# A ResNet-with-attention pair on one NeuronCore: another queue for the first input, lent rooms for weights, another projection order, halved last products

## The chip, the cores and the metric

The kernel runs on one core of a Trainium2 chip. The metric is the device time of one execution in microseconds (us), as the median of three runs. One more execution is recorded by the hardware profiler; its trace has a span of its own, which starts and ends with the first and last instruction of the program.

## The reference

Two bottleneck blocks on 16 images of 1024 channels and 32 x 32 pixels, all float32. The first block has local self-attention over 3 x 3 neighbours (32 heads of 8 channels) in its middle, the second has a plain 3 x 3 convolution:

```
# block 0
h = relu(bn(conv1x1(x, w_conv1)))                     # 1024 -> 256
q, k, v = relu(bn(conv1x1(h, wq))), relu(bn(conv1x1(h, wk))), bn(conv1x1(h, wv))
attn = softmax_k(einsum('bgdhw,bgdkhw->bgkhw', q, unfold3x3(k) + pos))
a = relu(bn(einsum('bgdkhw,bgkhw->bgdhw', unfold3x3(v), attn)))
x1 = relu(bn(conv1x1(a, w_conv3)) + x)                # 256 -> 1024
# block 1
y = relu(bn(conv1x1(x1, w1)))                         # 1024 -> 256
y = relu(bn(conv3x3(y, w2)))                          # 256 -> 256
out = relu(bn(conv1x1(y, w3)) + x1)                   # 256 -> 1024
```

## The kernel before, in words

An image is a sequence of stages, and the stages of the 16 images stand in one list (`stages`, made from the words `P0 P1 ... U15`). C is the first 1x1 convolution (`first_conv`, L1058), Q and V are the projections (`project`, L443), F is the last 1x1 of block 0 fused with the first 1x1 of block 1 (`fused`), W is the 3x3 convolution of four images by Winograd's form (`winograd_conv`), U is the last 1x1 (`last_sum`; for images 12 to 15 `late_sums` with Strassen's seven products on a quarter of the output each, `Pair`). `P0` stands for C0 Q0 V0. The list begins `P0 P1 P2 P3 C4 F0 Q4 V4 F1 P5 P6 F2 P7 F3 C8 Q8 W0 V8 ...` and ends `F12 F13 F14 U10:0123 F15 U10:4567 U11:01234 W12 U11:567 U12 U13 U14 U15`.

TensorE (PE) runs the stages in that order. A float32 matrix product appears in the trace as two MATMUL passes, so 6240 passes are 3120 products. PSUM holds four tiles of 128 x 1024 (`psum`, `bufs=4`), which ScalarE empties (L423 for F and U, L471 for q, k and v, L512 for the position product) and also fills in advance with the residual (L395, `seed`). VectorE computes the attention (L603 to L682), Winograd's transforms (L734 to L745), and in W the sums of the products. The engines execute what they are given in program order, each its own.

What VectorE does between the stages, and with it the order on the other engines' queues, is written out by hand: `ORDER` has a word for each part of a stage, and each letter of a word emits one step: `j` a step of attention, `e` the exponentials (on ScalarE, L642), `f` a step of the transforms in front (at first Winograd's transform of the weights, `winograd_weights`), `m` a move, `a` ReLU of attention's result (L709), `w` ReLU of Winograd's result (L893). Before any `e`, `j` steps have made the logits; L635 subtracts their maximum.

DMAs are issued from three queues. SyncE (SP) loads weights (`more_weights`, L131) and stores k and v with a halo (L483), transformed weights (`uw`, L289) and transformed images (`v`, L770). GpSimd (POOL) loads x, residuals and transformed images (`more_loads`, L344) and stores results (L424). ScalarE loads the parameters `par` (L92), and that is its first instruction. All of x, the two halves of the first chunk among them, is loaded by GpSimd's queue.

Weights have five rooms of 128 x 1024 (`wpool`). A new piece is asked for when an old one is used up (`done_with`), from a list in the order of use (`queue`). The 3x3 convolution has 18 pieces U of 512 KB, and PE takes each for 8 products.

In `project` the order is k, q, v by halves n = 0, 1. For `together(b)` (images from 4 on, where V follows Q at once) it is k0 k1 q0 q1 v0, then the position product (L504), then v1; else k0 q0 q1 k1, position product, v0 v1. Where a fused stage or U follows, the two residual seeds of that stage are put into PSUM tiles before v0/position and before v1.

At the very end `late_sums` runs `Pair` objects, one per quarter of the output channels. For the last two pairs (`end`) products 2 and 3 go to PSUM banks that already hold the rest of the sum, so that only the last step of the result (bias and ReLU) and the store follow.

Of the kernel before, what the change touches and what calls it, by code (L numbers as in the profile page):

```python
# [72 lines left out]
def sa_bottleneck_kernel(ctx: ExitStack, tc: tile.TileContext, x, w1t, wqkvt, w3t, u1t, u2t, u3t, params, out):  # L73
# [15 lines left out]


    par = const.tile([P, _NPAR], F32, tag="par", name="par")
    nc.scalar.dma_start(par, params)  # L92


    uw = dram.tile([NI, 3, P, NW, 2, WID], F32, tag="uw", name="uw")
# [18 lines left out]
    def more_weights():  # L114

        if not queue:
            return
        key = name, of, half = queue.pop(0)
        t = wpool.tile([P, HW], F32, tag="w", name=f"{name}{half}_{of[0]}")
        src = source(name, half)  # L120
        n, k = src.shape[-1], 1
        for d in src.shape[1:-1]:
            k *= d
        view = t[:, : k * n].rearrange("p (c n) -> p c n", n=n)
        if len(src.shape) == 4:
            view = t.rearrange("p (m j o) -> p m j o", m=NW, j=2)
        if of[1] == 0 and name == "w1":
            for part in (slice(0, 1), slice(1, k)) if half == 0 else (slice(0, k),):
                nc.sync.dma_start(view[:, part], src[:, part])
        else:  # L130
            nc.sync.dma_start(view, src)  # L131
        pieces[key] = view

    def done_with(key):

        if last_use[key] == now[0]:
            more_weights()

    now = [0]

# [172 lines left out]
    def more_loads():  # L313

        while loads and live[0] < CHUNKS + RESULTS - 1:
            kind, b, c = loads[0]
            late = kind == "r" and b >= B - NK

            spare = kind == "x" and b < 2 and c >= CHUNKS
            if live[0] >= CHUNKS and not (kind == "x" and b < 2) and not (late and late_rooms):  # L320
                return
            if kind == "V":

                if forms.get((b, c[1] == 2), 0) < NK:
                    return
                src = form_room(b)[c[0], c[1]].rearrange("p k j e -> p (k j e)")
            elif kind == "r":
                if (b, c) not in stored:
                    return
                src = stored[b, c]  # L330
            else:
                src = x[b, c * P : (c + 1) * P, :]
            name = f"{kind}_{b}_{c}".translate(str.maketrans(" ,", "__", "()"))
            if late and live[0] >= CHUNKS:
                t = late_of[loads[0]] = late_rooms.pop(0)
                live[0] -= 1
            elif spare:
                t = rpool.tile([P, HW], F32, tag="r", name=name)
            else:
                t = xpool.tile([P, NK * 2 * PART], F32, tag="x", name=name)  # L340
                t = t if kind == "V" else t[:, :HW]

            for part in ((slice(0, HALF), slice(HALF, HW)) if loads[0] == ("x", 0, 0) else (slice(None),)):
                nc.gpsimd.dma_start(t[:, part], src[:, part])  # L344
            loaded[loads.pop(0)] = t
            live[0] += 1

# [543 lines left out]
    def finish_winograd(b, n):  # L891
# [4 lines left out]
        )  # L896

    ORDER = (
        ". . f . ff f . fff . . ff f . ff . . . ff ffff j ff jj j . j . j . . jj jj . jj jj . . . e j j j j "
        "jj j j jj j j j . jjjj . . j j . j j . a j j j j j j e j . . jj jj . jjj jmj j . . j . jj . j . . jj "  # L900
        ". . f aj ff . . . jf . . . j fjj jj j fj j . ej jj j jm j . mfj . . j j . jj . jj j f f f f . jf . j "
        "f j fj j . . j j j j ajj j . j e . jjj m jj j m j j j . j j . jjj . jj . . . jj j . j jf . f f . afj "
        "j f j . . . jj ffj e . jjj j mmjj . j . jj . . . . . jj f j f . f fff . jjjf . . . . jj . . j j . . "
        ". . . j . . . . . . . . . . j jw j j jw j j ejj j j . j jmm j jww . j j jj . jj . j j j j . j j jww "
        ". jj j j j jejj ja mjww m j j j . j . jj . j . j . jj j . jja . j jj . . j j j jj . j jejj m . jjm . "
        ". j ja j . f . ff f j f j . fjf . . . . . jj j jj j . ff a f f j f j . fjf . . . . j . j jjj . f f f "
        "f j j ff jejj . jf m . ff . ffm . f f j fj . j j . j . j j j j jj j . j j . j . . jj . . j . j . . . "
        "j . . . . . . . . . . . jwj j je jjjw . mj mj j . jj . . j jww . j jjj . j j . j j j . j . jj jww j "
        "jj j ejajj . mj jj w mw jj . j . j j j jj j . . . j j j a j j j j jj . j jje jj j . jm m j . j j j . "
        ". j f f f f j f j . fjjjf . . . j j . j j f f ff . aj . f j . . . j fj jjf j j je a jjj . . j mj . . "  # L910
        "j . jmj . j . jj j . jjf . . f . f f jf . . jff . jf . ff . . . f fff j j j . . . j jj j j . . . . j "
        ". . . . . . . . j . . ejj j mwwj m jjj . . . j j j . j jww jj j . j jj . . j j j . jjaj . j jww jej "
        "jj m . j mj . j ja . . j jj . j j jj j j . . . . j j . jj . j j ajj j j je jjj . j j . . . j . j jj "
        ". . j j jf . f . ff j f . ffffffffwf a . ff . . w . . . . . . . ff . . fff . . . . . . . ff ff . . . "
        "f . f . f . . . . . . . . . . . . . . . . . . . ww w w w w . w . w . . . . . . . . . "
    )

    class Side:
# [100 lines left out]

    def together(b):  # L1020
        at = [(kind, c) for kind, c, of in stages].index(("qk", b))
        return b >= 4 and stages[at + 1][0] == "v"

    def weights_of_stage(kind, b, of):
        if kind == "conv1":
# [134 lines left out]
    def late_weights():  # L1160
# [4 lines left out]
        for half in range(2):  # L1165
# [7 lines left out]
        blocks["s"] = s  # L1173
        rooms = [
            apool.tile([P] + shape, F32, tag=tag, name=tag).rearrange("p d w -> p (d w)")
            for tag, shape in (("bnv", [HEAD_DIM, HALO]), ("bnk", [HEAD_DIM, HALO]), ("qc", [HEAD_DIM, JPIX]),
                               ("pc", [NPOS, JPIX]))
        ]
        rooms.append(kp.rearrange("p n r w -> p (n r w)"))
        hidden_ = vh.rearrange("p r w -> p (r w)")  # L1180
        for k, t in enumerate(rooms[:3] + rooms[4:]):
# [21 lines left out]
    class Pair:  # L1203
# [18 lines left out]
        def product(self, i):  # L1222
# [8 lines left out]
            nc.tensor.matmul(ps, w, by, start=i in (1, 2, 7) and not (i == 2 and self.end), stop=True, skip_group_check=True)  # L1231
            if i == 1 or (i == 2 and not self.end):
                self.add(0, 0, ps)
                if self.end:
                    nc.scalar.activation(self.banks[2], self.r[0][:, :HALF], AF.Identity)
            elif i == 6:
                self.add(1, 0, ps)
            elif i == 5:
                if self.end:
                    self.add(0, 1, ps)  # L1240
                    if self.last:
                        nc.vector.tensor_copy(self.banks[3], self.r[0][:, HALF:])
                    else:
                        nc.scalar.activation(self.banks[3], self.r[0][:, HALF:], AF.Identity)
                    self.add(1, 1, ps)
                else:
                    self.add(1, 1, ps)
                    self.add(0, 1, ps)
# [3 lines left out]
                self.add(1, 0, ps)  # L1252
            elif i == 3 and not self.end:
                nc.scalar.activation(self.r[0][:, HALF:], ps, AF.Identity)

        def result(self, m):
            o = 2 * self.q + m
# [4 lines left out]
            if self.end:  # L1262
# [3 lines left out]
                    nc.scalar.activation(t_, r_, RELU, bias=shift, scale=1.0)  # L1266
                    nc.gpsimd.dma_start(to, t)
                elif m == 1:
                    nc.scalar.activation(t_[:, two], r_[:, two], RELU, bias=shift, scale=1.0)
                    nc.vector.tensor_scalar(t_[:, one], r_[:, one], shift, 0.0, ALU.add, ALU.max)  # L1270
                    nc.sync.dma_start(to, t)
                elif not self.last:
                    for i, part in ((2, one), (3, two)):
                        ps = self.banks[i].rearrange("p (j n) -> p j n", j=2)
                        nc.scalar.activation(t_[:, part], ps, RELU, bias=shift, scale=1.0)
                    nc.sync.dma_start(to, t)
                else:
                    ps = [self.banks[i].rearrange("p (j n) -> p j n", j=2) for i in (2, 3)]
                    nc.scalar.activation(t_[:, one], ps[0], RELU, bias=shift, scale=1.0)
                    nc.vector.tensor_scalar(t_[:, two], ps[1], shift, 0.0, ALU.add, ALU.max)  # L1280
                    nc.scalar.dma_start(to[: P // 2], t[: P // 2])
                    nc.sync.dma_start(to[P // 2 :], t[P // 2 :])
            else:
                nc.scalar.activation(t_, r_, RELU, bias=shift, scale=1.0)
                nc.gpsimd.dma_start(to, t)
# [4 lines left out]
    def late_sums():  # L1290
# [8 lines left out]
        for b in range(B - NK, B):  # L1299
            steps = iter(())  # L1300
            for q in range(NC // 2):
# [5 lines left out]
                if last_one:  # L1307
                    last_one.product(5)
                    for m in (1,) if last_one.end else range(2):
                        last_one.result(m)  # L1310
                if this.last:
                    order = (6, 7, 5, 4)
                elif this.end:
                    order = (7, 6, 4)
# [4 lines left out]
                if this.last:  # L1319
                    last_one.product(2)  # L1320
                    last_one.product(3)
                    this.result(1)
                    last_one.result(0)
                    this.product(2)
                    this.product(3)
                    this.result(0)
                else:
                    for _ in range((0, 1, 2, 1)[q]):
                        next(steps, None)
# [8 lines left out]
    def run(at):  # L1338
# [3 lines left out]
        for after in stages[at : at + 3]:  # L1342
            if after[0] == "fused":
                next_fused[0] = after[1]
                break
        fetch_attended()
        if kind == "fused":
            parts, count = fused(b, of, then), 2 * NC
        elif kind == "u3" and b >= B - NK:
# [35 lines left out]
    def at_first():  # L1385
        more_weights()
        more_loads()
        more_weights()
        norms()
        load_taps(0)  # L1390
# [55 lines left out]
```

## Time and profile before

| | |
|---|---|
| median of 3 runs | 2380.18 us (2379.92 to 2381.85) |
| profiled execution, its own time | 2377.51 us |
| its span in the trace | 2375.8 us, at a granted TensorE clock of 0.999 |
| PE busy | 2350.4 us (99%), 6240 passes |
| DVE (VectorE) busy | 2163.3 us (91%) |
| ACT (ScalarE) busy | 932.8 us (39%) |
| POOL busy | 492.0 us (21%) |
| DMA | 691.11 MB, 291 GB/s over the span |

PE is the engine named in 88% of the chain that ends last. Its busy time counts matmul passes whose ends are modelled. The step from the start of one pass to the start of the next is the better measure: 0.429 us for a pass of 512 columns and 0.216 us for one of 256, wherever nothing holds PE up. A longer step is a stall, and the stalls can be added up from the timeline.

### The profile page before, as it was taken

Reading aid. Unit: us, or ns where it says so; the run is one execution under the profiler, and the core shown is the slowest. Engines: PE = TensorE matmul, PEld = TensorE weight load, DVE = VectorE, ACT = ScalarE, POOL = GpSimd, SP = SyncE. Lnnn points to the kernel's source line nnn. Section 1 sums busy time; section 2 is a strip of 40 time slices with the busy share of each in tenths; the row PEclk is TensorE's granted clock in tenths of the full one; section 3 lists DMA queues with packets and bytes.
Section 4 is the critical chain, followed back from the end, with each engine's and each line's share of the span. In section 5 each row is a group of like instructions: output and inputs, shape, how many; then the busy total and the mean of one; then the engine's idle time right before and its main releaser. Section 6 shows DMA issues by size and latency. Waiting matters only on the chain.

```text
span 2375.8 us, 18829 instructions
## 1 busy us (share of the span) xinstructions
PE 2350.4 (99%) x6240; PEld 1142.1 (48%) x6240; DVE 2163.3 (91%) x1784; ACT 932.8 (39%) x889; POOL 492.0 (21%) x903
## 2 busy tenths in 40 slices
PE   8999999999999999999999999999999999999998
PEld 3444444444476444444466444444467444444843
DVE  4989999999989999999899989999989989975687
ACT  3322342323122574433122574324222463354277
POOL 3211121212121232111111232112111231111222
PEclk9999999999999999999999999999999999999999
DMA  9967786877797998687888998678788897698988
GB/s 341 382 223 265 276 276 248 279 279 263 268 329 243 338 396 316 221 266 238 254 310 271 326 381 326 219 274 288 261 293 295 309 369 248 214 345 288 332 296 292
DMA packets 294769, 691.11 MB, mean 291 GB/s; under 512 B 20752, under 2 KB 164624, under 8 KB 285968
## 3 DMA queue, kind: packets, MB, share of 16 engines
q0 software_dynamic: 120192, 472.19, 54.6%
q1 hardware_dynamic: 174256, 217.41, 28.1%
q8 instruction: 50, 0.82, 0.1%
q14 instruction: 47, 0.39, 0.0%
q10 hardware_dynamic: 224, 0.31, 0.0%
HBM read 414.79 MB, written 275.03 MB: 290 GB/s over the span
## 4 chain that ended last, share of the span: by engine, by line
PE 88%; DVE 6%; DMA 2%; ACT 1%; issue 0%; SPq 0%; ACTq 0%; DVEq 0%
PE ps L372 35%; PE ps L404 28%; PE ps L458 13%; PE ps L805 8%; PE ps L1231 4%; DMA U<-uw 2%; DVE prod L603 1%; DVE acc L660 1%; DVE acc L678 1%; DVE prod L608 0%; ACT kp L471 0%; DMA v<-v 0%; PE ps L504 0%; DVE form L734 0%; DVE z L831 0%
## 5 line engine op out<-in xcount | busy, mean ns | idle before, releaser
L372 PE MATMUL ps<-result,u 128*128 128x512 f32 x1024 | 458.4, 593 | 0.1
L404 PE MATMUL ps<-a,w 128*128 128x512 f32 x1024 | 457.8, 593 | 0.0
L372 PE MATMUL ps<-x,w 128*128 128x512 f32 x1024 | 444.3, 595 | 7.8 <-DMA x<-in_x_dram 7.5
L660 DVE TENSOR_TENSOR acc<-e,bnv 128x2048 f32<-128x2048 f32 x144 | 327.5, 2283 | 27.5 <-ACT e L642 24.4
L404 PE MATMUL ps<-y,u 128*128 128x512 f32 x768 | 331.1, 592 | 0.0
L603 DVE TENSOR_TENSOR prod<-qc,bnk 128x2048 f32<-128x2048 f32 x144 | 324.1, 2287 | 1.8
L423 ACT ACTIVATE result<-ps,par 128x1024 f32<-128x1024 f32 x128 | 142.4, 1113 | 452.6 <-PE ps L404 379.6
L372 PEld LDWEIGHTS ps<-x,w 128*128 128x128 f32 x1024 | 195.6, 191 | 253.2 <-issue 242.8
L372 PEld LDWEIGHTS ps<-result,u 128*128 128x128 f32 x1024 | 194.7, 190 | 245.5 <-issue 236.4
L404 PEld LDWEIGHTS ps<-a,w 128*128 128x128 f32 x1024 | 195.0, 190 | 244.5 <-issue 243.7
L678 DVE TENSOR_TENSOR acc<-acc 128x2048 f32<-128x2048 f32 x128 | 293.4, 2292 | 4.4
L404 PEld LDWEIGHTS ps<-y,u 128*128 128x128 f32 x768 | 146.3, 190 | 182.9 <-issue 180.9
L458 PE MATMUL ps<-h,wqk 128*128 128x512 f32 x512 | 222.3, 593 | 0.0
L424 POOL DMA_DIRECT2D r<-result x128 | 68.7, 537 | 600.7 <-ACT result L423 574.3
L608 DVE TENSOR_TENSOR prod<-prod 128x2048 f32<-128x2048 f32 (+1 forms) x80 | 166.2, 2077 | 2.3
L458 PEld LDWEIGHTS ps<-h,wqk 128*128 128x128 f32 x512 | 97.5, 190 | 122.3 <-issue 110.7
L423 ACT ACTIVATE result<-ps,bn_sh 128x1024 f32<-128x1024 f32 x96 | 106.7, 1112 | 107.2 <-PE ps L404 105.6
L1070 ACT ACTIVATE h<-ps,par 128x1024 f32<-128x1024 f32 x32 | 38.4, 1203 | 270.7 <-PE ps L372 270.7
L471 ACT ACTIVATE kp<-ps,par 128x1024 f32<-128x1024 f32 x64 | 77.4, 1210 | 150.2 <-PE ps L458 118.2
L395 ACT ACTIVATE ps<-s 128x1024 f32<-128x1024 f32 x128 | 131.2, 1025 | 12.7 <-DMA s<-in_x_dram 10.2
L344 POOL DMA_DIRECT2D x<-in_x_dram x129 | 68.7, 534 | 285.8 <-PE ps L372 221.8
L828 ACT ACTIVATE z<-ps 128x1024 f32<-128x1024 f32 x48 | 49.2, 1024 | 183.7 <-PE ps L805 140.7
(381 smaller groups left out, 2679.0 us busy)
## 6 DMA issues: line engine op xcount, KB each, us to landing
s<-in_x_dram POOLq DMA_DIRECT2D x128, 512.0 KB, 6.1
r<-result POOLq DMA_DIRECT2D x128, 512.0 KB, 4.5
x<-in_x_dram POOLq DMA_DIRECT2D x127, 512.0 KB, 5.2
out_dram<-result POOLq DMA_DIRECT2D x125, 512.0 KB, 6.4
r<-r POOLq DMA_DIRECT2D x111, 512.0 KB, 6.9
v<-v SPq DMA_DIRECT2D x96, 408.0 KB, 4.6
U<-uw SPq DMA_DIRECT2D x72, 512.0 KB, 5.1
bnk<-kp SPq DMA_DIRECT2D x32, 680.0 KB, 6.2
```

The costliest lines, as they stand in the source:

```text
L372: nc.tensor.matmul(ps[n][:, halves(half)], wt[:, c % (NC // 2), n * P : (n + 1) * P], src[:, halves(half)], start=(c == first), stop=(c == ...
L395: nc.scalar.activation(ps, loaded.pop((self.kind, self.b, o)), AF.Identity)
L404: nc.tensor.matmul(self.ahead[o][:, halves(half)], pieces[key][:, n, o % (NC // 2) * P :][:, :P], self.src[:, n, halves(half)], start=Fals ...
L423: nc.scalar.activation(to_, ps, RELU, bias=self.shift(o), scale=1.0)
L458: nc.tensor.matmul(ps[:, halves(half)], pieces[key][:, m, at : at + P], h[:, m, halves(half)], start=(m == 0), stop=(m == NW - 1),)
L471: nc.scalar.activation(dst, src, func, bias=col(f"L0_conv_{name}_b", n), scale=col(f"L0_conv_{name}_s", n),)
L603: nc.vector.tensor_tensor(by_row(t[:, two]), by_row(qc), kc[:, :, i : i + JROWS, j : j + W], ALU.mult)
L608: nc.vector.tensor_add(u[:, :, 0:4], u[:, :, 0:4], u[:, :, 4:8])
L660: nc.vector.tensor_tensor(by_row(dst), rows(e[:, k, :]).unsqueeze(1).to_broadcast([P, HEAD_DIM, JROWS, W]), vc[:, :, i : i + JROWS, j : j ...
L678: nc.vector.tensor_add(acc, acc, t)
L805: nc.tensor.matmul(acc[i][:, at, :, n, :], pieces[key][:, m, at, n * P : (n + 1) * P], v[:, at, :, m * (TILES + TR) :][:, :, :TILES], star ...
L1231: nc.tensor.matmul(ps, w, by, start=i in (1, 2, 7) and not (i == 2 and self.end), stop=True, skip_group_check=True)
```

## The change

Five edits:

1. The two halves of chunk 0 and all of chunk 1 of image 0's x are loaded by ScalarE's queue, ahead of the parameters; GpSimd's queue begins with chunk 2.
2. `lend_rooms`, called at the start of stage U10:4567, lends four rooms of 128 x 1024 to U pieces of the last Winograd stage: two in the tile `qc`, which the last logits have read, and two in `kp`, which the last v has left. `more_weights` puts U pieces there while such a room is spare, and `done_with` gives the room back.
3. `together` is true only where V is followed by C, or by U of Winograd's group: images 5, 9, 10, 12 and 15. Images 4, 6, 7 and 13 go over to k0 q0 q1 k1, position, v0 v1. The wv piece is loaded again for images 4 and 7.
4. The last pair's products 2 and 3 are done in halves of pixels (`split_ends`, `split_result`): four products of 256 columns instead of two of 512, in the order 2, 3, 2, 3, into four PSUM tiles. ScalarE and VectorE finish each half as it comes; the first half of the pixels is stored by SP while the second is finished. `result(1)` of the last pair goes wholly to VectorE (before: half ScalarE, half VectorE), and comes after the pair before's `result(0)`.
5. `ORDER` is revised. Most words move by one place or none.

```
-    nc.scalar.dma_start(par, params)
...
+        if spare and name[0] == "U":
+            t = lent[key] = spare.pop(0)
+        else:
+            t = wpool.tile([P, HW], F32, tag="w", name=f"{name}{half}_{of[0]}")
...
         if last_use[key] == now[0]:
+            if key in lent:
+                spare.append(lent.pop(key))
+                if not queue or queue[0][0][0] != "U":
+                    return
             more_weights()
+    def lend_rooms():
+        late_room["qc"] = apool.tile([P, HEAD_DIM, JPIX], F32, tag="qc", name="qc").rearrange("p d w -> p (d w)")
+        for t in (late_room["qc"], kp.rearrange("p n r w -> p (n r w)")):
+            spare.extend([t[:, :HW], t[:, HW : 2 * HW]])
+        for _ in range(len(spare)):
+            if queue and queue[0][0][0] == "U":
+                more_weights()
...
-                nc.gpsimd.dma_start(t[:, part], src[:, part])
+            by = nc.scalar if loads[0] in (("x", 0, 0), ("x", 0, 1)) else nc.gpsimd
+            for part in (halves(0), halves(1)) if loads[0] == ("x", 0, 0) else (slice(None),):
+                by.dma_start(t[:, part], src[:, part])
...
-        return b >= 4 and stages[at + 1][0] == "v"
+        return b > FIRST and [kind for kind, c, of in stages[at + 1 : at + 3]] in (
+            ["v", "conv1"], ["v", "u3"]
+        )
...
+        def split_ends(self):
+            tiles = [self.banks[2], banks.tile([P, HALF], F32, tag="ps0", name="ps")]
+            tiles += [self.banks[3], banks.tile([P, HALF], F32, tag="ps1", name="ps")]
...
+            for n in range(2):
+                nc.scalar.activation(self.split[2, n], self.quarter(self.r[0], 0, n), AF.Identity)
+        def split_result(self):
...
+            for n in range(2):
+                for i in (2, 3):
+                    nc.tensor.matmul(
+                        self.split[i, n], weights[i], self.quarter(y[:, 1], i - 2, n),
+                        start=False, stop=True, skip_group_check=True,
+                    )
+            for n in range(2):
+                at = slice(n * HALF // 4, (n + 1) * HALF // 4)
+                nc.scalar.activation(t_[:, 0:2, at], self.split[2, n], RELU, bias=shift, scale=1.0)
+                nc.vector.tensor_scalar(t_[:, 2:4, at], self.split[3, n], shift, 0.0, ALU.add, ALU.max)
+                if n == 0:
+                    nc.sync.dma_start(to[:, halves(0)], t[:, halves(0)])
+            nc.scalar.dma_start(to[: P // 2, halves(1)], t[: P // 2, halves(1)])
+            nc.sync.dma_start(to[P // 2 :, halves(1)], t[P // 2 :, halves(1)])
...
+                nc.vector.tensor_scalar(t_, r_, shift, 0.0, ALU.add, ALU.max)
...
+        if kind == "u3" and not late_room and any(s[0] == "wino" and s[1] == B - NK for s in stages[at + 1 : at + 3]):
+            lend_rooms()
```

`ORDER` by stage, where the prediction speaks of it (one word after each part of the stage; W has one more before its first part):

```
        before                               after
C0      .  .  f  .  ff f  .  fff             .  .  f  .  ff .  f  ff
Q0      .  .  ff f  .                        .  .  f  ff ff
V0      ff .                                 .  .
C1      .  .  ff ffff j  ff jj j             f  .  fff fj ffff . jj j
C4      j  j  j  j  j  j  e  j               a  j  jj .  j  j  j  e
Q4      .  f  aj ff .                        .  f  j  f  fa
W0      .  .  j  j  .  .  .  .  .  j  ...    .  jj .  j  .  .  .  .  .  j  ...
```

What this makes of ScalarE's order in the built programs: in Q0 the two q's (L471) come after two steps of the weights' transform in place of three, and k1 after one more; image 1's exponentials (the pair e_1) come after both halves of image 4's hidden layer (L1070) and not before the second residual seed. On SP the order around W0 is the same; at the end the four lent loads stand before the last image's stores of `v`.

## Prediction

> **What bounds the kernel now.** I read the page's slices first (PE at 9 tenths from the second slice on, clock full), then PE's timeline, start to start. Where PE is never held, 128x512 passes start 0.429 us apart. All 6240 passes at such steps (0.216 for 256 columns, 0.054 for a position pass) make 2336.3 us. The span of 2375.8 is that plus 7.5 before the first pass, 25.2 of stalls, and 7.2 from the last pass's start on, less its own step. The change removes no pass, so it can only touch these 39.5 us.
>
> The list of waits names what holds PE up:
>
> ```profile
> PE ps L372 <- DMA x<-in_x_dram: 7.5, 1, 7.5
> PE ps L805 <- DMA U<-uw: 5.2, 3, 2.6
> PE ps L458 <- ACT kp L471: 2.3, 7, 0.3
> PE ps L504 <- ACT q L471: 1.6, 1, 1.6
> PE ps L1231 <- ACT result L423: 1.3, 1, 1.3
> ```
>
> (total us, times, longest). One by one in the timeline, with what a stall adds to the step: start 7.5, and 1.96 more in the first four pairs of passes, which step 0.85; position product of image 0 (52.45) 3.66, where images 1 to 3 have 1.02; conv of image 1 (62.8) 0.5; v1 after the position product of images 4, 6, 7, 9, 12, 13, 15: 0.87 each, where 5 and 10 have 0.47; F2's second part (475) 0.44; W0's third U pair (684.4) 3.9; W12 (2200.7 and 2213.9) 2.82 and 0.82; the last pairs 1.1.
>
> Last I looked at who else is full. The table by stretches shows VectorE with hardly any idle time between 160 and 573 us (columns: length, PE, PEld, DVE, ACT, POOL busy, clock, DMA share, GB/s):
>
> ```profile
> 160.00:210.00 50.00, 50.00 (x131) 21.72 (x130) 49.28 (x27) 9.36 (x8) 9.20 (x16) 1.00 0.68 222
> 210.00:314.00 104.00, 103.67 (x256) 45.52 (x255) 102.36 (x67) 39.55 (x36) 17.89 (x33) 1.00 0.79 276
> 468.00:573.00 105.00, 104.66 (x257) 45.63 (x256) 103.29 (x70) 32.37 (x29) 18.29 (x34) 1.00 0.74 256
> ```
>
> So time won by PE before 160 us counts later only if VectorE wins it too.
>
> **The change part by part.**
>
> *First x by ScalarE.* Issues of the first stretch (queue, count, KB, median us from issue to landing):
>
> ```profile
> x<-in_x_dram POOLq DMA_DIRECT2D x2, 256.0 KB, 6.5
> w<-in_w1t_dram SPq DMA_DIRECT2D x1, 384.0 KB, 3.6
> par<-in_params_dram ACTq DMA_DIRECT2D x1, 48.0 KB, 2.5
> w<-in_w1t_dram SPq DMA_DIRECT2D x1, 128.0 KB, 2.3
> ```
>
> The Trainium skill (DMA: Bandwidth & Descriptors, Rules for kernel authors) speaks against this: spreading DMAs over issuing engines only saves issue time, for all share the same 16 engines. By it the gain is 0.5 us: POOL issues at 1.34, ScalarE at 0.81. The rows say more, since the engines were not full then: 7 GB/s to 2 us, 265 from 2 to 4. POOL's half needs 6.15 us to land; SP's 384 KB issued 0.07 us earlier need 3.56. A 256 KB half on ScalarE, between 2.4 and 3.6 plus what w takes beside it, lands at 3.8 to 5.2; I take 4.4. PE starts 3.1 earlier (bounds 2.3 and 3.7; 0.5 by the rule). The second half and chunk 1 follow in time: the slow pairs take 3.4 us, chunk 1 is due 5.2 after the start, and 1 MB at 265 to 411 GB/s is there by 7. Chunks 2 on come from POOL at about 2.2 us each, PE takes 3.43. `par` lands some 4 us later; its first hard reader on PE's path is h at 35. ScalarE's three extra issues, about 0.45 each, stand before a wait for weights until 14.4. SP's w and g share with one queue more until about 8 us, so the taps come up to 1.8 later.
>
> *Order of ScalarE in Q0.* q0 waited 5.54 us for a landing, because its room had held the fourth transformed row of weights (issued 40.85, 10.3 to land). Now two rows stand before it, and it takes the third's room, landed at 38.1. The 3.66 becomes 1.02: 2.6. Behind q1 ScalarE waits for the fourth row (about 49.5), then k1 and one group of taps; the fifth row (issued about 42, landing 55) comes before `by_offset`, done about 56.3 where PE needs it at 57.1. The 0.5 goes too: 3.1 together. Bounds: 1.5 if that landing is late, 3.2 at most. Stage C1 then starts 6.2 earlier. x for C2 has landed at 103.4 to 110.2, due from 105.2 on by 3.43 steps: covered.
>
> *The exponentials of image 1.* VectorE's stream restarts at 142.5 on e_0, for which it had waited 8.4 us; ScalarE had been held by PE's h there, so 6.2 passes on. But e_1 now stands behind h of image 4:
>
> ```profile
> 236.35 1.06 ACT L642 ACTIVATE e<-e 128x1024 f32<-128x1024 f32 x1 [5.98 <-DVE e L635]
> 237.75 1.27 ACT L642 ACTIVATE e<-e 128x1280 f32<-128x1280 f32 x1 [0.34 <-DVE e L635]
> 238.93 1.01 ACT L395 ACTIVATE ps<-s 128x1024 f32<-128x1024 f32 x1
> 239.88 2.28 ACT L1070 ACTIVATE h<-ps,par 128x1024 f32<-128x1024 f32 x2
> ```
>
> Before, the first e was ready at 237.41 and VectorE, at 237.63, did not wait. Now PE ends C4 at 231.3, h ends at 232.65, e at 233.7; VectorE is ready at 231.5. It waits 2.2 us, and is only 4.0 ahead. Queued behind it are all of VectorE's attention steps. PE meets this at F2: there e_3 waits for VectorE and holds back the first result, which PE already missed by 0.1 us (stall 0.44). So PE falls back to VectorE's lead: minus 2.2, and what images 4 and 6 gain (below) is lost with it. Bounds: 0 (if VectorE is late at 231.5 for another reason, or its stream closes up) and 2.2.
>
> *k, q, v order.* In images 4, 6, 7, 13 v1 waited for the room of v0 (ACT kp, 0.40 each). In the new order v1 takes the position product's room, emptied 1.1 us after it while v0 runs 3.43. The position product waits for q1, which k1's 3.43 covers (1.21 for L471). Gain 0.4 at 7 and 13, 0 at 4 and 6: 0.8 (bounds 0 and 1.6). Two wv loads of 256 KB are hidden: SP issues them behind `a`'s store some 25 us before use.
>
> *Lent rooms.* W12 starts at 2194.0 and waits at 2200.7 for U11, issued only at 2188.9, behind VectorE's `v` stores on SP. The lent four are issued behind U20, about 2158; from 2165 to 2180 the DMA share is 0.47 to 0.73, so about 2 MB fit. U's 2.82 and 0.82 vanish. What is late next is the image side. These issues stood at 2188.4 and 2203.0:
>
> ```profile
> v<-v SPq DMA_DIRECT2D x1, 408.0 KB, 14.0
> ...
> V__2_8329<-v POOLq DMA_DIRECT2D x1, 544.0 KB, 6.1
> ```
>
> That last store lands at 2202.4 and V__2 at 2209.1, while PE without a wait wants it at 2207.8: 1.3 us of new stall, nothing having left that stretch of the queues (U30 takes U11's place). 3.64 less 1.3 is 2.3 (upper bound 3.6, if the store lands earlier). A rule bears on what is left: the Trainium skill (TensorE: Matmul & The Clock Gate, The HAM clock gate) has the clock halved after an idle window of about 3.4 us, so neither wait of W0 and W12 should cost it. The trace agrees for 2.7 us in W12 and not for 2.2 us in W0, after which the clock was 0.57 for 4 us and cost 1.7. By the rule 1.3 us costs itself only; by W0's row up to 1.7 more, so the lower bound is 0.6.
>
> *The last products.* PE's end stays at 2369.2. Before: VectorE's half until 2370.4, ScalarE's, held up by its share of result(1), until 2371.04; stores at 2371.06. Now ScalarE does the previous pair's two (1.02 each) by 2368.6 and its own halves (0.42, as other rows of 256) by 2369.5. VectorE: result(1) of 1024 columns about 1.25 from 2367.6, then two halves to 2369.8. Stores at 2369.85, 1.2 earlier, half as large but behind the first half's: 0.4. Together 1.6 (bounds 1.0 and 2.0).
>
> *The rest of ORDER*: 0, as the steps on each engine keep nearly their order. ScalarE's `a` mostly move later by a part, further from their landings. W0 keeps its SP order: its U stands behind k1's store and took 15.2 us at a DMA share above 1, so 3.9 stays.
>
> Sum: 3.1 + 3.1 - 2.2 + 0.8 + 2.3 + 1.6 = 8.7. Span 2367.1, profiled execution 2368.8 instead of 2377.51; the runs' median was 2.7 above that, so 2371.5.
>
> **Rivals.** *The lead survives* (0.26): VectorE does not lose 2.2, so images 4 and 6 count as well: 8.7 + 2.2 + 0.8 = 11.7, 2368.5; if W0's wait of 3.9 goes too, 2364.6. For it: VectorE has waits for stores (4.0 us once before 480) that may shrink. Against: the position of e_1 in the built order. *The lead is given back to the DMA* (0.20): the share is 1.02 to 1.06 from 50 to 110 us, and stores of weights need 10 to 16 us there. PE 6 us early meets h or k waiting for rooms at C1's end, losing 4: 2375.5, next to no change. *Slower* (0.04): the same place, but ScalarE stands in order before h of image 1 for the ninth row's landing. I expect that row issued near 66 and landed by 82, PE needing h at 83. It costs us for us once later than that. To be 0.2% slower it must eat 8.7 + 4.8 = 13.5 us, so land after 96, twice the longest such row (15.7). That an edit does nothing is excluded: the built order shows ScalarE's x and U in qc and kp.
>
> **How the numbers follow.** Likeliest (0.50): 2371.5. A difference within 0.2%, 4.8 us, is about what a measurement can't tell from none. Range 2364.5 to 2376: down to the surviving lead with W0, up to the lead given back. Faster 0.86 (0.50 + 0.26 + half of the second rival), same 0.10, slower 0.04.
>
> **What would show it.** First pass near 4.4; position product of image 0 without a wait for q; C1 near 55; VectorE waiting about 2 us on e_1; F2's stall about 3.4; 0.47 after the position product of 4, 6, 7, 13; no PE wait for U in W12, one near 1.3 for V; the last stores 1.2 after PE's end. Wrong if x lands after 6, or a new ScalarE wait stops PE between 55 and 110.

## The result and the profile after

The changed kernel takes 2369.35 us (median of 5 runs, 2367.12 to 2372.3) against 2380.18: a ratio of 0.9955, 95% interval 0.994 to 0.9969. The forecast was 2371.5. The profiled execution took 2369.26 us with a span of 2367.5, which is 8.3 us less than the span before. As spans, the sum had promised 2367.1. Its total is right, but five of its terms are wrong, and they cancel.

PE's waits in the changed kernel (total us, times, longest) stand beside those of before:

```profile
PE ps L390 <- DMA x<-in_x_dram: 4.8, 1, 4.8
PE ps L823 <- DMA V__2_2527<-v: 2.1, 1, 2.1
PE ps L823 <- issue: 1.3, 1, 1.3
PE ps L1252 <- ACT result L441: 1.3, 1, 1.3
PE ps L476 <- ACT kp L489: 1.0, 3, 0.3
```

The first pass starts 2.7 us sooner. Three waits for kp are left of seven, and q is gone from the list. The two L823 lines are W0 and W12. The name in W0's line misleads: V__2_2527 landed at 682.7, after PE had gone on at 681.40. Two things ended just before that. A U issued at 666.0 landed at 680.73, after 14.7 us. ScalarE's copy `z`, which empties the PSUM tile that PE writes next, ended later still, at 681.34:

```profile
680.32 1.02 ACT L846 ACTIVATE z<-ps 128x1024 f32<-128x1024 f32 x1 [6.82 <-DMA pos<-by_offset]
```

`z` takes a room (tag "z") that `by_offset` had held, and had to wait until the stores of `by_offset` had landed (the last at 680.10). Before the change the U ended last: it landed at 686.66, PE went on at 686.79, and `z` had ended at 685.46. So the U alone explains all but the last 0.5 us of W0's wait here. In the other traces one or the other comes last.

Added up from start to start, PE's excess over its steps (to which the first pass's start is added) shows where the 8.3 us came from. Each column is one execution; how much the rows of the start, W0 and W12 differ between executions of one kernel is shown under after_again below.

| stretch | before | after | won | predicted |
|---|---|---|---|---|
| start to 40 us (first x) | 9.50 | 7.38 | 2.1 | 3.1 |
| 40 to 66 (q and by_offset of image 0) | 3.61 | 1.83 | 1.8 | 3.1 |
| F2 and what e_1's wait does there | 0.44 | 0.00 | 0.4 | -2.2 |
| v1 of images 4, 6, 7, 13 | 4 x 0.40 | 0 | 1.6 | 0.8 |
| W0 | 3.92 | 4.01 | -0.1 | 0 |
| a stall at 1495 | 0.32 | 0 | 0.3 | 0 |
| W12 | 3.64 | 1.59 | 2.0 | 2.3 |
| the last products and stores | 6.76 | 6.64 | 0.1 | 1.6 |
| sum | | | 8.2 | 8.7 |

(The last row runs from the last pass's start plus its own step to the span's end.)

ScalarE's list of waits between 36 and 62 us (to 66 before), first before, then after, shows that the wait for a row of weights in front of q has not gone:

```profile
ACT q L471 <- DMA uw<-u: 5.5, 1, 5.5
```

```profile
ACT q L489 <- DMA uw<-u: 6.4, 1, 6.4
```

VectorE does wait for image 1's exponentials, as forecast. In ScalarE's timeline they stand behind image 4's h (start, us, engine, line), and VectorE's next step shows the idle time before it:

```profile
231.95 1.21 ACT L1091 ACTIVATE h<-ps,par 128x1024 f32<-128x1024 f32 x1 [1.82 <-PE ps L390]
233.67 1.21 ACT L1091 ACTIVATE h<-ps,par 128x1024 f32<-128x1024 f32 x1 [0.51 <-PE ps L390]
234.77 2.20 ACT L660 ACTIVATE e<-e 128x1024 f32<-128x1024 f32 x2
```

```profile
235.85 4.50 DVE L678 TENSOR_TENSOR acc<-e,bnv 128x2048 f32<-128x2048 f32 x2 [2.01 <-ACT e L660]
```

But F2 shows no stall. Between the two places VectorE got back twice what it had lost. VectorE's lists of waits up to 700 us have these lines, before and then after:

```profile
DVE acc L660 <- ACT e L642: 8.4, 1, 8.4
DVE form L734 <- DMA a<-acc: 4.0, 1, 4.0
```

```profile
DVE acc L678 <- ACT e L660: 3.7, 2, 2.0
DVE tree L642 <- DMA pos<-by_offset: 2.8, 1, 2.8
```

The wait of 4.0 us for the store `a<-acc` is gone, and so is most of the 8.4. VectorE's timeline shows why the store is no longer waited for, before and after:

```profile
396.86 2.29 DVE L680 TENSOR_TENSOR acc<-acc,se 128x2048 f32<-128x2048 f32 x1
399.07 4.49 DVE L603 TENSOR_TENSOR prod<-qc,bnk 128x2048 f32<-128x2048 f32 x2
407.56 1.50 DVE L734 SCALAR_TENSOR_TENSOR form<-vh 128x612 f32<-128x612 f32 x2 [4.01 <-DMA a<-acc]
```

```profile
395.61 2.29 DVE L698 TENSOR_TENSOR acc<-acc,se 128x2048 f32<-128x2048 f32 x1
397.82 1.50 DVE L752 SCALAR_TENSOR_TENSOR form<-vh 128x612 f32<-128x612 f32 x2
```

`acc`, `prod` and `form` take turns in the same rooms (tag "t"). Before, the logits took the free room, and `form` had to wait until `acc`, which was being stored, left the other. In the revised `ORDER`, three steps of the transform (words of C5) come first and take the free room. That is one step of attention (`j`) moved behind three steps of the transform (`f`), within an edit that the prediction had put at nothing.

### The profile page after: what moved, and what is told of

Its sections match the earlier page's. It is cut to its first block, busy times and chain, and to the rows that moved or that the text cites. A ratio compares the mean times of both kernels' runs of the same rounds, so it can differ in the third digit from the quotient of the medians.

```text
span 2367.5 us, 18845 instructions
## 1 busy us (share of the span) xinstructions
PE 2349.7 (99%) x6244; PEld 1140.3 (48%) x6244; DVE 2163.1 (91%) x1786; ACT 932.0 (39%) x890; POOL 492.1 (21%) x900
## 4 chain that ended last, share of the span: by engine, by line
PE 96%; DVE 1%; DMA 1%; ACT 1%; issue 0%; ACTq 0%; DVEq 0%; SPq 0%
PE ps L390 37%; PE ps L422 32%; PE ps L476 13%; PE ps L823 9%; PE ps L1252 4%; DMA uw<-u 1%; PE ps L522 1%; DMA V__2_2527<-v 0%; DVE z L849 0%; DVE y L849 0%; DVE prod L621 0%; DMA x<-in_x_dram 0%; ACT kp L489 0%; DVE z L853 0%; ACT y L911 0%
```

## The experiments

Each starts from the changed kernel. "Span" is that of the profiled execution (2367.5 for the changed kernel); medians are of 4 to 20 runs (end_no_store has one); ratios are to the kernel before on the same chip.

**form_after_logits.** The three steps of the transform stand behind the logits again, as before the change.

```
- jjf ffj          (last two words of C5)
+ jj  jfff
```

> The changed kernel, but three steps of image 2's transform in the words of C5 stand again behind one step of logits. Theory: the revised order took a wait of 4.0 us for a store off VectorE there, and that paid for the 2.0 us that VectorE newly waits on image 1's exponentials. With the step put back VectorE waits about 4 us for its room near 406 us, its lead over the kernel before shrinks from 5.5 to 1.5 us, and PE, 4.7 ahead there, stalls 3.5 us in F2 near 475 us. That is not given back later: span 2371.0, median 2372.9. Rival (these words are worth nothing, PE isn't tied to VectorE at F2): no stall in F2, median 2369.4.

Span 2369.1, median 2370.86, ratio 0.9967 (0.9955 to 0.998). VectorE's wait and F2's stall are back:

```profile
404.48 1.50 DVE L752 SCALAR_TENSOR_TENSOR form<-vh 128x612 f32<-128x612 f32 x2 [1.84 <-DMA a<-acc]
```

```profile
PE ps L390 <- ACT result L441: 1.8, 1, 1.8
```

Idle time is 1.8 us in place of 4, and F2's stall 2.3 in place of 3.5, but the chain is the forecast one. VectorE finishes e_3 at 469.96, in the changed kernel at 467.56. ScalarE's first result starts 1.2 us after e_3 in both. VectorE's delay of 2.4 became 2.3 of PE.

**exps_earlier.** The exponentials of image 1 go back ahead of h: last words of C4 `j e` become `je .`.

> The changed kernel, but image 1's exponentials stand one word earlier, ahead of image 4's hidden layer on ScalarE as in the kernel before. Theory: VectorE does not wait for them (0 to 0.3 us in place of 2.0), but PE has room at F2 already, so nothing else moves: span 2367.5, median 2369.4. Rival (PE follows VectorE throughout, as the prediction had it): 2.0 us faster, median 2367.4.

VectorE does not wait at 235 us and has e_3 ready 3.4 us sooner than in the changed kernel, but PE gains nothing at F2, where its stall is zero already. Instead VectorE waits 2.0 us there:

```profile
DVE acc L678 <- ACT e L660: 2.0, 1, 2.0
```

The span is 2364.2 and the median 2365.79 (ratio 0.9945, 0.9932 to 0.9959), 3 us below the changed kernel's span. Of that, 2.15 are W0, 0.7 is the start and 0.9 is W12, and 0.4 is lost in a new stall at 1463. after_again below shows that the first three places differ between executions of one kernel, so a gain by the edit is not shown.

**both_words_back.**

> The changed kernel with both words put back: image 1's exponentials earlier and image 2's transform behind the logits. Theory: VectorE wins 2.0 at the one place and loses 4.0 at the other, so its lead at F2 is 3.5 us against PE's 4.7, and PE stalls about 1.6 us there: span 2369.1, median 2370.9. Rival (only one of the two words matters): 3.5 us of stall, or none.

Span 2367.0, median 2368.7, ratio 0.9961 (0.9947 to 0.9974). F2 stalls 2.1 us (forecast 1.6). VectorE comes 2 us sooner to `form` and waits 4.8 there, and both versions go on at 404.4: the store's landing sets the time, so leads in front of it do not add.

**x_by_gpsimd.** The first x goes back to GpSimd's queue, the parameters first on ScalarE's.

```
-            by = nc.scalar if loads[0] in (("x", 0, 0), ("x", 0, 1)) else nc.gpsimd
+            by = nc.gpsimd
```

> The changed kernel, but the first x by GpSimd's queue and the parameters first on ScalarE's, as before. Theory: the first pass is at 7.5 us in place of 4.8 and four slow pairs follow in place of six, so PE is 2.1 us later at 12 us; but the third row of weights then lands no later, so the position product of image 0 and the taps' wait before by_offset cost 1.0 to 1.4 less, and only 0.7 to 1.1 us is left of it at the end: span 2368.4, median 2370.2. Rival (all of it is carried to the end): 2.1 to 2.7 us, median 2371.5 to 2372.

The first pass is at 7.9 us, and at 40 us PE is 2.9 behind the changed kernel. But q waits for no row:

```profile
ACT h L1091 <- PE ps L390: 4.8, 2, 4.3
ACT q L489 <- PE ps L476: 3.2, 2, 2.2
ACT u L292 <- DMA uw<-u: 3.2, 2, 2.7
```

From 40 to 66 us it loses 0.35 in place of 1.83, and at 160 us it is 1.45 behind (forecast 0.7 to 1.1; the rival, all of it, 2.1 to 2.7). So first x and the new order of Q0 share one gain. The order alone takes 3.3 of the 3.6 us between 40 and 66; with x by ScalarE, half of x's 2.9 us is lost there again. The size is not sharp: the eight other executions with x by ScalarE and this order of Q0 lose 1.4 to 2.6 us there, and at 160 us x_by_gpsimd is 0.4 to 2.2 behind them. Span 2369.9, median 2367.11, ratio 0.9952 (0.9938 to 0.9965): a difference of 1.5 us cannot be read from these times.

The loss comes through SP's loads of taps. The first three land at 21.3 us (before 16.7; 19.8 here), the third row is stored at 35.0 (before 30.5; 33.6 here) and lands at 47.2 (before 38.1; 39.6 here). q takes that row's room. The changed kernel's list of SP's waits up to 8 us has a wait for x:

```profile
SPq L273 <- DMA x<-in_x_dram: 2.0, 1, 2.0
SPq L133 <- DMA w<-in_w1t_dram: 0.9, 1, 0.9
```

SP neither issues nor reads x, but the semaphores in the trace show the link. The loads of SP and ScalarE signal their landing on eight semaphores in turn, those of GpSimd on eight others, and a load waits until the one that had its semaphore before has landed. With three x loads on ScalarE's queue, SP's second load of taps is the ninth. It signals on semaphore 99, like the first half of x, and is issued at 4.79, when that has landed (4.77). Before, it was issued at 2.81, and the ninth was the fourth load of taps.

This wait did not make the taps late. The first load of taps, issued at 2.26 in both kernels, lands at 16.7 us in place of 12.2, and the next two follow 2.3 us apart in both. What changed is the share of SP's queue. From 6 to 14 us the queues of GpSimd (q0), SP (q1) and ScalarE (q10) moved (packets, MB, share of the engines), before and then after:

```profile
q0 software_dynamic: 488, 1.77, 56.1%
q1 hardware_dynamic: 677, 1.37, 46.1%
```

```profile
q0 software_dynamic: 554, 2.02, 64.4%
q1 hardware_dynamic: 554, 0.62, 22.0%
q10 hardware_dynamic: 279, 0.54, 17.5%
```

That cannot be all of it: in x_by_gpsimd SP's queue moved 1.34 MB, and the taps still land 3.1 us later than before. Why is open. The third row then takes 12.2 us to land in place of 7.6 (6.0 here). It is issued just after GpSimd has begun to load the next image's x, at 34.4 us (before 40.3, 38.9 here); that this is what slows it was not tried.

**kqv_from_4.** `together` is again `b >= 4 and stages[at + 1][0] == "v"`.

> The changed kernel, but k, q, v order as before (together for every image from 4 on whose V follows Q). Theory: v1 waits again for v0's room behind the position product of images 4, 6, 7 and 13, 0.40 us each and 1.6 together, all carried to the end, since PE and not VectorE sets the pace at F2 now: span plus 1.6, apart from what the clock does in W0 (0 or 1.75). Rival (as predicted, the share of images 4 and 6 is swallowed at F2): plus 0.8.

The span is 2376.3, the median 2377.52, the ratio 0.9992 (0.9985 to 0.9999). v1's stalls of images 4, 6, 7 and 13 are back with 0.40 each. The rest is a miss, a wait that neither theory had:

```profile
PE ps L476 <- DMA wqk<-in_wqkvt_dram: 5.7, 1, 5.7
```

In this mixture the wqk of image 4 is asked for only at 282.0, behind SP's store of `acc`, and lands at 293.7, when PE has waited 5.8 us. Slow passes after it cost another 2.4. In the changed kernel wqk is issued at 233.7 and in the kernel before at 258.2. The order of k, q, v decides when a room of weights is freed, and the words of `ORDER` are fitted to it. So the 1.6 us is this edit's direct effect only, and its whole price can't be told by undoing it alone. Nor can the run tell the theory from the rival: with that stall PE comes to F2 too late to meet VectorE.

**no_lent.** `spare.extend([])` in place of the two halves of each room.

> The changed kernel without lent rooms (no room is put on the list of spare ones). Theory: PE waits for U in W12 again, 2.7 and 0.8 us, and the wait for V of 1.5 us, which that hides, goes: plus 2.0 us. Rival (V is late anyway and ends last in either kernel): within 0.5 us of the changed kernel.

Span 2366.8, median 2369.71, ratio 0.9963 (0.9952 to 0.9975). W12 loses 3.2 us, to U:

```profile
PE ps L823 <- DMA U<-uw: 2.7, 2, 1.7
```

With lent rooms the twelve traces lose 0.0 to 4.4 there, 1.3 on the mean, by V's landing. 3.2 and 3.6 (before) less 1.3 is about 2.1. That may be too much. In no_lent the V landed at 2204.99, only 0.8 us before the U that PE waited for. Had PE not stood 1.2 us for a U before that, it would have waited 2.2 us for this V, and about 0.9 us would be left as the edit's worth. So V is nearly as late as the rival had it, and the times (2369.71 and 2369.35) show no difference.

**whole_end.** The last pair's end as before.

> The changed kernel with the last pair's end as before (two whole products, result(1) in two halves on two engines ahead of the pair before's result(0)). Theory: in both versions the program ends when the last 1.5 MB of stores are drained, which takes 6 us from the first of them on; the trace from the last full-width pass to the end grows by 0.1 to 0.4 us only. Rival (as predicted, the last store's issue sets the end): plus 1.6 us.

**end_no_store.** The store of the last pair's result(1) is cut to 8 numbers.

```
-                    nc.sync.dma_start(to, t)
+                    nc.sync.dma_start(to[:1, :8], t[:1, :8])
```

> The changed kernel, but of the last pair's result(1) only 8 numbers are stored in place of 512 KB (the output lacks that part). Theory (the drain of the last stores sets the end): with 0.5 MB less ahead of them the last stores land 1.0 to 1.3 us sooner after their issue (2.8 to 3.1 us in place of 4.1 to 4.7), and the span's tail after the last pass goes from 6.9 to 5.7. Rival (each store has its own fixed time of about 4 us): the tail stays at 6.9.

From the last pass's end to the span's end it is 6.96 us in whole_end (span 2364.7, median 2366.65, ratio 0.9948, 0.9933 to 0.9963), 6.64 in the changed kernel, 5.13 in end_no_store (span 2366.9, one run of 2368.6). The last issues with their KB and us to landing, for whole_end, the changed kernel and end_no_store:

```profile
out_dram<-result SPq DMA_DIRECT2D x2, 512.0 KB, 2.6
out_dram<-result SPq DMA_DIRECT2D x1, 256.0 KB, 3.2
out_dram<-result ACTq DMA_DIRECT2D x1, 256.0 KB, 3.9
```

```profile
out_dram<-result SPq DMA_DIRECT2D x2, 512.0 KB, 3.1
out_dram<-result SPq DMA_DIRECT2D x1, 256.0 KB, 4.7
out_dram<-result ACTq DMA_DIRECT2D x1, 128.0 KB, 4.4
out_dram<-result SPq DMA_DIRECT2D x1, 128.0 KB, 4.1
```

```profile
out_dram<-result SPq DMA_DIRECT2D x1, 512.0 KB, 2.6
out_dram<-result SPq DMA_DIRECT2D x1, 256.0 KB, 2.6
out_dram<-result ACTq DMA_DIRECT2D x1, 128.0 KB, 2.8
out_dram<-result SPq DMA_DIRECT2D x1, 128.0 KB, 3.1
```

The halves do finish sooner (0.9 us after PE in place of 2.0), but in the changed kernel 1.5 MB is issued within 1.8 us, where whole_end spreads it over 2.7. Each store is issued into the ones before it. Take 0.5 MB away and the same halves land 1.0 to 2.1 us sooner after their issue. The last of them is also issued 0.5 us sooner after PE's end, since SP's issue of the store ahead of it takes 0.35 us in place of 0.73. So 1.5 MB of stores set the end, through their landing and through SP's queue. Halves with result(1) stored early, as before, would keep the finish and spread the stores; that was not run.

**after_again, warm, fewer_rows, warm_fewer_rows.** The changed kernel once more; with PE busy from 1.5 us on a blank tile; with two steps of the weights' transform moved from C0 and Q0 into C1; with both.

```
+    blank = kp.rearrange("p n r w -> p (n r w)")[:, :HALF]
+    nc.vector.memset(blank, 0.0)
+    warm = psum.tile([P, HW], F32, tag="ps", name="ps")
+    for _ in range(4):
+        nc.tensor.matmul(warm[:, : HALF // 2], blank[:, :P], blank[:, : HALF // 2], start=True, stop=True)
```

```
     C0                       Q0               C1
-    . . f . ff . f ff        . . f ff ff      f   . fff fj ffff . jj j
+    . . f . ff . f f         . . f f ff       fff . fff fj ffff . jj j
```

> The changed kernel once more, unaltered, to see what its own stalls do from one execution to the next. Theory: the start (first pass 4.2 to 4.9, slow steps), W0 (0.8 to 4.2) and W12 (0.7 to 4.4) wait for transfers whose landings differ between executions; every other stall repeats within 0.1 us. Rival: they differ between kernels only, and this run repeats the first: 4.0 in W0, 1.6 in W12.

> The changed kernel with four products of 256 columns on a blank tile ahead of everything on PE, so that PE is busy from about 1.5 us on. Theory: the clock is full about 5 us after PE's first work, so the slow steps on x go from 2.5 to below 1.0; chunk 1 of x, landed at 9.7, then holds PE, so 1.1 to 1.5 us is won at 12 us; the third row of weights does not land sooner, so the wait for q in image 0 grows by as much and 0 to 0.4 us is left at 100 us. Rival (what is won at the start is carried through): 1.1 to 1.5 us at 100 us.

> The changed kernel with one row of the weights' transform fewer ahead of q0 on ScalarE and one fewer ahead of by_offset (two steps moved from C0 and Q0 into C1). Theory: q0 takes the room of a row that landed at 37, not 47 us, so the position product of image 0 costs 0.35 to 0.8 in place of 1.3, and by_offset holds nothing up (0 in place of 0.5): 0.8 to 1.3 us won at 66 us. Rival (the rows pile up in C1 and ScalarE is late with h of image 1 at 79 us): a new stall of 1 to 4 us between 66 and 100 us.

> Both of them. Theory: without the wait for the third row the start's gain is carried on: 2.0 to 2.6 us won against the changed kernel at 100 us, 1 us more than the two alone give. Rival: the next transfer takes it back (stall between 66 and 110 us), 0.5 to 1 us won.

| kernel | PE behind at 40 us | at 100 us | W0 | W12 | span | median | ratio |
|---|---|---|---|---|---|---|---|
| changed kernel | 7.4 | 9.5 | 4.0 | 1.6 | 2367.5 | 2369.35 | 0.9955 (0.994 to 0.9969) |
| after_again | 7.0 | 8.8 | 1.6 | 2.8 | 2366.0 | 2367.68 | 0.9961 (0.9949 to 0.9973) |
| warm | 7.1 | 9.5 | 0.3 | 0.7 | 2363.4 | 2365.78 | 0.9951 (0.9938 to 0.9964) |
| fewer_rows | 7.3 | 8.7 | 1.3 | 0.0 | 2362.4 | 2365.94 | 0.9954 (0.994 to 0.9969) |
| warm_fewer_rows | 6.9 | 8.7 | 1.8 | 1.0 | 2364.2 | 2366.09 | 0.9953 (0.9942 to 0.9965) |

(PE's excess as above; the 1.7 us that the blank products take is counted as lost.) after_again differs from the changed kernel's first execution at the start, in W0 and in W12. It also loses 0.4 us less between 40 and 66 us and 0.3 us more at F2: PE, 0.8 us further ahead, meets VectorE there, so the margin at F2 is small. Over the five kernels that are the same up to W0 (the changed kernel twice, no_lent, whole_end, end_no_store), W0 costs 4.0, 1.6, 2.0, 1.9 and 0.8. A span of one execution therefore says nothing under 3 us, and the four ratios cannot be told apart.

warm: at 12 us PE is 6.3 us behind, 0.6 to 1.0 less than the changed kernel's two executions, but four executions without the blank products stand at 6.3 to 6.5 too, so a gain by the warm clock is not shown. h takes it back at 34 us, since ScalarE has a step of the transform in front of it. At 40 us nothing is left. fewer_rows: q and by_offset hold nothing up (0.35 from 40 to 66), but the rows pile up ahead of h of image 1, where 0.7 us more is lost: both theories were right in part, and 0.1 to 0.8 us remains. Both together are no better. With x by ScalarE all twelve traces stand between 6.9 and 7.6 us at 40 us, as if the path had a floor there: behind x stands h, behind h the taps. No version was shown to beat the changed kernel.

## Why the prediction was right or wrong

*First x by ScalarE.* The first pass at 4.8 (4.2 to 4.8 in the runs) for 4.4, and a gain of 2.7 us, above the skill's 0.5: the same half of x landed 3.96 us after its issue on ScalarE's queue and 6.15 on GpSimd's. The rule spoke of issue time, and the row (6.15 against 3.56 us to land) was the better guide. Two steps failed. The slow steps, left at 1.96, became 2.6 us, so 2.1 reached 40 us. An earlier start is not shown as the reason: up to 12 us the other executions with x by ScalarE lose 1.7 to 3.0 us, x_by_gpsimd 2.4. And "the taps come up to 1.8 later" was 4.6: sharing with one queue more was the right mechanism, but part of the size (3.1, which x_by_gpsimd has too) is open.

*Order of ScalarE in Q0.* "It takes the third's room, landed at 38.1" failed. The room was right, but its landing was read from the kernel before and not moved with the taps: 47.2. So q still waits, and x_by_gpsimd, where the row lands at 39.6, shows that without this it would not. by_offset did not get its gain either: ScalarE waits for the fifth row, landed at 58.05, up to 58.1 (0.5 as before). 1.8 in place of 3.1. The bound of 1.5 "if that landing is late" holds it.

*The exponentials.* The wait was sized well (2.0 for 2.2), and PE does meet VectorE at F2. The step that failed is "the rest of ORDER: 0": a move in C5 took off a wait of 4.0 us on the same engine, ahead of the same meeting point. form_after_logits shows that without it F2 stalls 2.3 us. The rival "the lead survives" had named this very wait as one that might shrink, and it was the rival's mechanism that came true. For the same reason images 4 and 6 counted.

*k, q, v order.* 0.40 at each of four images, as worked out, and all of it kept.

*Lent rooms.* 2.0 for 2.3: no wait for U in W12, and a V next late with 1.5 for 1.3. That the sizes agree is luck. The V that the sum had late (V__2_8329, here V__2_8328) landed at 2199.4, 2.4 us before PE wanted it: counted from the start of W12, the store ahead of it landed 2.0 us sooner than before and its own load took 4.5 us in place of 6.1. PE waited for the next one, V__2_8375, which stood behind three stores of results on GpSimd's queue (one before), was issued at 2197.0 and landed at 2206.6. The double price that a halved clock would have had didn't come.

*The last products.* The results were ready 1.1 us earlier after PE's end, for 1.2 in the sum. The step that failed is "stores at 2369.85, 1.2 earlier, half as large but behind the first half's: 0.4": on PE's shifted time the last store was issued only 0.5 earlier, behind SP's issue of the store before, and took 4.1 us to land against 3.8. Moving result(1) behind the other result bunched the stores, and of the 1.6 us 0.1 was left.

*From span to median.* The 2.7 us added to get from the profiled execution to the median came from one execution that was quick. The changed kernel's profiled time lies 0.1 under its median. Without it the sum gives 2368.8, with it 2371.5; the measured 2369.35 lies between.

The misses were -1.0 and -1.3 at the start, +2.6 at F2, +0.8 for k, q, v and -1.5 at the end. That they cancel is chance.

## What to carry to other kernels

When an order written by hand is revised, look at every room that two kinds of work share: which of them takes the free one is worth as much as the edits that have a name. Two gains that lie in a row on one path are one gain if a transfer behind them sets a floor; move that transfer's issue and landing with the edit before adding. A load that moves to another queue also takes a turn of that queue's landing semaphores, and a share of the engines from the queues that run beside it. At a kernel's end count the megabytes that are issued in the last microseconds, not only when the last one is issued.

## What was not expected of the hardware

A halved clock after a stall did not follow the stall's length. In W0, stalls of 2.04, 2.16, 2.22, 2.22 and 3.31 us were followed by 8 to 10 slow passes that cost 1.6 to 1.8 us; one of 2.11 by none; those of 1.80 and less by at most 0.35. In W12, 2.72 and 2.75 cost themselves only, and 2.93 was followed by slow passes of 1.4.

The traces' records of the granted clock show what it followed. They change only at whole multiples of 3.41 us from where the clock is first full (9.81 us in the changed kernel, 11.31 before). In W0 of the changed kernel PE's whole wait lies in one such stretch, and the next stretch is granted half (the 0.50). In both_words_back the 2.11 us fall on two stretches, 0.8 and 1.3, and the clock stays full:

```profile
678.82:682.24 3.42, 1.37 (x7) 0.89 (x6) 0.86 (x1) 1.02 (x1) 0.53 (x1) 1.00 1.02 419
682.24:685.65 3.41, 3.41 (x10) 2.67 (x9) 3.38 (x5) 1.02 (x1) 0.00 (x0) 0.50 1.02 409
```

```profile
678.57:681.98 3.41, 2.74 (x13) 2.08 (x11) 0.49 (x1) 1.02 (x1) 0.48 (x2) 1.00 1.01 358
681.98:685.40 3.42, 2.14 (x10) 1.93 (x11) 3.39 (x5) 1.02 (x1) 0.16 (x1) 1.00 1.03 414
```

(Columns as in the prediction's table by stretches.) So it is in all fourteen traces from the first full clock on: where PE stood still for 2.1 us or more of one stretch, counted from step to step, the next was at half, in seven cases; where it stood for 1.9 us or less, in none. (Left out are stretches that are themselves at half, and those of the position products, whose short passes do not tell PE's idle time.) The 2.72 and 2.75 of W12 split into 1.75 and about 1, and 2.35 of the 2.93 lay in one stretch. One stretch at half costs half of 3.41 us, 1.7. So whether a wait of 2 to 3 us costs double depends on where it falls, and that differs between executions.
